# Graph network of two layers: scatters without an order among themselves, list transpositions behind given messages, a small first piece

## The chip, the cores and the metric

The kernel runs on one core of one Trainium2 chip. The metric is the device time of one execution in microseconds (us). PE is the matrix engine, DVE the vector engine, ACT the scalar engine, POOL the general engine that also issues indirect transfers, SP the engine that issues most plain transfers. Each engine works through its own instructions in order and waits on semaphores.

## The reference

There are 6250 nodes with 256 features and 106250 edges, sorted by target; the last edge of each target is its loop. Each edge has one of two kinds. Layer 0 sends a message over each edge, sums the messages at the target, and passes the sum through gates and three small layers; layer 1 is graph attention with four heads. After each, the input is added and the row normalized.

```python
S = feat[src]
def edge_nn(x, W, b):
    h = relu(x @ W.T + b)
    return relu(h @ W.T + b)
msgs = where(rel == r, edge_nn(S, W_rel[r], b_rel[r]), msgs)   # r = 0, 1
agg = segment_sum(msgs, dst)
i, f, g, o = split(agg @ W_ih.T + b_ih + b_hh, 4)
c = sigmoid(i) * tanh(g)
hn = sigmoid(o) * tanh(c)
x0 = layernorm(x + mlp3(hn))
# layer 1: edges and a further loop for each node
h = (x0 @ W).reshape(n, 4, 64)
e = leaky_relu(a_src[src] + a_dst[dst], 0.2)
alpha = exp(e - m[dst]) / (denom[dst] + 1e-16)      # softmax over each target's edges
y = segment_sum(h[src] * alpha, dst) + bias + x0
out = layernorm(x0 + relu(layernorm(y) * gamma + beta))
```

## The kernel before, in words

A message depends only on the source node and the kind of the edge. So the kernel first makes the messages of every node for both kinds, and then gathers them by edge. It has three stages. The line numbers here are those of the kernel before.

**The first stage**, in `gnn_kernel`, does two things at once that do not depend on each other.

*The messages.* The 49 blocks of 128 nodes are taken in chunks of four (line 1132). For a chunk, SP loads the features turned (`fxc`, three buffers), PE does the first stage of the messages (L1143: two kinds, two halves of the features out, two halves in, so eight matmuls over up to 512 columns into `fph`), and ACT writes ReLU of it into `fhT` (L1150). Then for each block PE does four matmuls (L1157) into `fpm`, of which there are two buffers; DVE adds the bias (L1165) into `fms`, of which there are three; ACT takes ReLU (L1168), and SP stores the block in the table `parts` (L1170). The trace records each of these matmuls as two.

*The list.* The gathers need the list of edges without the loops. The edges lie in 7 groups of 126 runs of 128. DVE closes each run up over its loops by shifts of 1, 2, 4 ... 64 places (`frame` and `moved`, lines 878 to 902), and works out where the three blocks of each run go (`place`). POOL scatters them: 7 groups of 3 blocks make 21 indirect transfers into `packed` (L931). SP reads the closed list back from `packed` (`both` and `low_2`, lines 961 to 970, six transfers). DVE takes it apart again (lines 992 to 1048, here called the list operations): source row, target, kind, and the place where a target begins. PE turns five such arrays with 35 transpositions (L1059) and spreads the window's first targets with one matmul (`low_p`, L1085); DVE copies the results into the tables of indices (`idx0`, `idx1`, `mark`, `first`, `slot`).

The order of the instructions on each engine in this stage is set by a scheduler when the program is built: it places the instructions by the dependences that it knows and by costs of its own. Two transfers that write the same array in DRAM are taken to depend on each other, unless the kernel says that they do not.

**The second stage** (`fast`, first half) is layer 0. POOL issues 782 gathers of 128 rows from `parts` (L1265), PE sums them by one-hot matmuls (L1622), and the gates and small layers run beside that, in an order written out by hand. It begins when all messages are stored: on ACT the copy of `mark` (L1643) waits for the stores, and the first gather waits for it.

**The third stage** (`fast`, second half) is the attention: 782 gathers from `rows` in the same way, the weights of the edges, and the sums (L1911). A second path, `general`, for edges that are not sorted, is in the program and is not run with these inputs.

Of the kernel before, what the change touches and what calls it, by code (L numbers as in the profile page):

```python
# [42 lines left out]
P = 128  # L43
# [6 lines left out]
NB = -(-N // P)  # L50
# [6 lines left out]
CHUNK = 4  # L57
# [5 lines left out]
def blocks_of(n, size):  # L63
    return [(i, min(size, n - i)) for i in range(0, n, size)]
BF16 = mybir.dt.bfloat16
WT = 7
TC = -(-(E - N) // P)
NW = -(-TC // WT)
SLOTS = 64
NG = NW // 2  # L70
CT = 18 * WT
# [3 lines left out]
NC = -(-EC // CT)  # L75
# [628 lines left out]
def gnn_kernel(  # L704
# [26 lines left out]
    nc = tc.nc  # L731

    def at(ap, offset, dims):
        return bass.AP(tensor=ap.tensor, offset=ap.offset + offset, ap=dims)

    def rows(ap, n):

        return at(ap, 0, [[0, P], [1, n]])
# [7 lines left out]
    packed = dram.tile([2 * BLOCKS, HB], I32, name="packed")  # L746
# [25 lines left out]
    with (  # L772
# [2 lines left out]
        tc.tile_pool(name="fmsgp", bufs=2, space=PSUM) as mps,  # L775
    ):
        WrT_s = mw.tile([P, 2, 2, D], F32, name="fWrT")
        nc.scalar.dma_start(WrT_s, WrT.rearrange("r (k p) f -> p r k f", p=P))
        brc = mw.tile([P, 2, 2], F32, name="fbrc")
        brr = mw.tile([P, 2 * D], F32, name="fbrr")  # L780
        with nc.allow_non_contiguous_dma(reason="bias vectors, one element a partition"):
            nc.scalar.dma_start(brc, br.rearrange("r (k p) -> p r k", p=P))
        nc.scalar.dma_start(brr, rows(br, 2 * D))
        zrow = mw.tile([1, D], F32, name="fzrow")
        nc.vector.memset(zrow, 0.0)
        nc.sync.dma_start(parts0[ZERO0 : ZERO0 + 1, :], zrow)

        with (
# [19 lines left out]
            rest = EC - (NC - 1) * CT  # L808
            whole = CT * P
# [69 lines left out]
            for b in range(7):  # L879
                s = 1 << b  # L880
# [44 lines left out]
            for b in range(3):  # L925
                nc.vector.tensor_scalar(
                    place[:, b, :], two_t, side, float(b), op0=OP.add, op1=OP.add
                )
            for k in range(NC):
                for b in range(3):  # L930
                    nc.gpsimd.indirect_dma_start(  # L931
                        out=packed,
                        out_offset=bass.IndirectOffsetOnAxis(ap=place[:CT, b, k : k + 1], axis=0),
                        in_=frame[:CT, k, b * HB : (b + 1) * HB],
                        in_offset=None,
                    )


# [15 lines left out]
            both = lp.tile([P, 2, NC, P + 1], I32, name="both")  # L954
            nc.gpsimd.memset(both[:, :, NC - 1, :], 0)
            low_2 = lp.tile([1, 2, NW + 1], I32, name="low_2")
            nc.gpsimd.memset(low_2, 0)
            rest = TC - (NC - 1) * CT
            for s in range(2):
                o = (s * BLOCKS + 1) * HB - 1  # L960
                nc.sync.dma_start(
                    both[:CT, s, : NC - 1, :],
                    at(packed, o, [[P, CT], [whole, NC - 1], [1, P + 1]]),
                )
                nc.sync.dma_start(
                    both[:rest, s, NC - 1, :],
                    at(packed, o + (NC - 1) * whole, [[P, rest], [1, P + 1]]),
                )
                with nc.allow_non_contiguous_dma(reason="the last edge before each window"):
                    nc.sync.dma_start(  # L970
                        low_2[:, s, 1:NW], at(packed, o + WT * P, [[0, 1], [WT * P, NW - 1]])
                    )

            low_r = lp.tile([1, NW + 1], I32, name="low_r")
# [2 lines left out]
            low = lp.tile([1, NW + 1], F32, name="low")  # L977
# [66 lines left out]


            dstE = lp.tile([P, COLS], F32, name="dstE")
            src0 = src1
            nc.vector.tensor_scalar(src0[:CT], src1[:CT], 1.0, None, op0=OP.subtract)
            for to, of in (
                (idx0, row),  # L1050
                (dstE, list_f[:, :, 1:]),
                (mark, rel_f[:, :, :P]),
                (idx1, src0),
                (first, steps),
            ):
                for k0, kn in blocks_of(NC, 4):
                    pt = lps.tile([P, 4 * CT], F32, name="turned")
                    for k in range(kn):
                        nc.tensor.transpose(  # L1059
                            pt[:, k * CT : (k + 1) * CT], of[:CT, k0 + k, :], ident[:CT, :CT]  # L1060
                        )
                    n = min(kn * CT, COLS - k0 * CT)
                    if to is not mark:
                        nc.vector.tensor_copy(to[:, k0 * CT : k0 * CT + n], pt[:, :n])
                        continue

                    to2, of2 = (
                        ap.rearrange("p (g j) -> p g j", j=2 * WT)
                        for ap in (mark[:, k0 * CT : k0 * CT + n], pt[:, :n])
                    )  # L1070
                    for a, b, c in ((0, 1, 0), (1, 2, WT), (2, WT + 1, 1), (WT + 1, 2 * WT, WT + 1)):
                        nc.vector.tensor_copy(to2[:, :, a:b], of2[:, :, c : c + b - a])
            ones = lp.tile([P, P], F32, name="fones")
# [8 lines left out]
            nc.vector.tensor_scalar(odd_i, odd[:, 6:7], 1.0, None, op0=OP.min)  # L1082

            low_p = lps.tile([P, NW + 1], F32, name="low_p", bufs=1)
            nc.tensor.matmul(low_p, ones[0:1, :], low, start=True, stop=True)  # L1085
            low_b = lp.tile([P, NW + 1], F32, name="low_b")
            nc.vector.tensor_copy(low_b, low_p)
            own = dstE[:, : NW * WT].rearrange("p (w j) -> p w j", j=WT)
# [31 lines left out]
            for w0, wn in blocks_of(NW, P // (WT + 1)):  # L1120
                pt = lps.tile([P, 4 * CT], F32, name="turned")
                n = wn * (WT + 1)
# [6 lines left out]
                    slots[w0 : w0 + wn, :].rearrange("w (j e) -> (w j) e", e=P), rel_b[:n, :]  # L1129
                )  # L1130

        for b0, bn in blocks_of(NB, CHUNK):
            cols = bn * P
            xc = mp.tile([P, 2, CHUNK * P], F32, name="fxc", bufs=3)
            nc.sync.dma_start(
                xc[:, :, :cols], xT[:, b0 * P : b0 * P + cols].rearrange("(k p) n -> p k n", p=P)
            )
            hT = mp.tile([P, 2, 2, CHUNK * P], F32, name="fhT")
            for r in range(2):
                for m in range(2):  # L1140
                    ph = mps.tile([P, CHUNK * P], F32, name="fph")
                    for k in range(2):
                        nc.tensor.matmul(  # L1143
                            ph[:, :cols],
                            WrT_s[:, r, k, m * P : (m + 1) * P],
                            xc[:, k, :cols],
                            start=(k == 0),
                            stop=(k == 1),
                        )
                    nc.scalar.activation(  # L1150
                        hT[:, r, m, :cols], ph[:, :cols], AF.Relu, bias=brc[:, r, m : m + 1]
                    )
            for j in range(bn):
                pm = mps.tile([P, 2, D], F32, name="fpm")
                for r in range(2):
                    for k in range(2):
                        nc.tensor.matmul(  # L1157
                            pm[:, r, :],
                            hT[:, r, k, j * P : (j + 1) * P],
                            WrT_s[:, r, k, :],  # L1160
                            start=(k == 0),
                            stop=(k == 1),
                        )
                ms = mp.tile([P, 2, D], F32, name="fms", bufs=3)
                nc.vector.tensor_add(  # L1165
                    ms.rearrange("p r f -> p (r f)"), pm.rearrange("p r f -> p (r f)"), brr
                )
                nc.scalar.activation(ms, ms, AF.Relu)  # L1168
                b = b0 + j
                nc.sync.dma_start(  # L1170
                    parts0[2 * b * P : 2 * (b + 1) * P, :].rearrange("(p r) f -> p (r f)", r=2),
                    ms.rearrange("p r f -> p (r f)"),
                )

    odd_v = nc.values_load_multi_w_load_instructions(
        odd_i,
# [845 lines left out]
```

## Time and profile before

| what | value |
|---|---|
| median of 10 runs | 2275.83 us (2272.63 to 2279.74) |
| the profiled execution | 2274.85 us |
| its span in the trace | 2272.7 us |
| first stage, to the first gather at 204.34 | 204.3 us: PE busy 181.4, DVE 110.8, ACT 68.8, POOL 27.0; granted clock 0.97 |
| second stage, to 1222 | 1017.7 us: PE busy 858.5, DVE 372.6, POOL 751.4; granted clock 0.92 |
| third stage, to the end | 1050.7 us: PE busy 511.7, DVE 752.5, POOL 747.4; granted clock 0.68 |

All times in the text are microseconds from the start of the span. In a line of the trace in order of time, the first number is the start, the second the time to the end of the (merged) instructions, then come engine, line, operation, written and read tile, shapes, and count; in brackets stands how long the engine was idle before, and what ended that. An engine's name with q is its instruction queue, which issues transfers. The time of the profiled execution lies 2.15 above its span: that is outside of what the trace shows. In the slices of the page a digit is the busy share of a fortieth of the span in tenths.

### The profile page before, as it was taken

The numbers are of one execution on the slowest core, as the hardware profiler recorded it, in microseconds if no ns is written. First come the engines' busy times: TensorE is split into PE (matmuls) and PEld (weight loads), VectorE is DVE, ScalarE is ACT, GpSimd is POOL, SyncE is SP. The second block draws the span as 40 slices with busy tenths as digits, with TensorE's granted clock in tenths as the row PEclk, the third lists the DMA queues.
The fourth block names the chain that finished last, engine by engine and source line by source line (L and its number), as shares of the span: only waits on it lengthen the run. The fifth ranks groups of instructions, "written<-read, shape, count | busy, mean of one in ns | idle before, by whom it ended". The sixth has DMA issues, their size and how long they took to land. (4 is left out here: it accounts for less than half of the span.)

```text
span 2272.7 us, 22029 instructions
## 1 busy us (share of the span) xinstructions
PE 1551.6 (68%) x5722; PEld 769.9 (34%) x5722; DVE 1235.9 (54%) x3332; ACT 506.9 (22%) x1525; POOL 1525.8 (67%) x1603
## 2 busy tenths in 40 slices
PE   8987788887888888888992354554545545454563
PEld 5654233333333333333451232222323223232332
DVE  7452134334333343333542577677776877777786
ACT  3322012221222212222342112211111111212111
POOL 1213777777777777777773777777777777777760
PEclk9988799999999899999996676766767677676766
DMA  5335435554455544555553555555555555555550
GB/s 160 123 95 150 134 112 170 167 159 145 143 169 164 158 145 145 168 166 163 172 163 92 144 156 149 154 144 157 152 147 163 145 156 152 149 158 148 151 142 26
DMA packets 163393, 332.53 MB, mean 146 GB/s; under 512 B 42451, under 2 KB 74290, under 8 KB 163257
## 3 DMA queue, kind: packets, MB, share of 16 engines
q0 software_dynamic: 75968, 208.00, 33.6%
q1 hardware_dynamic: 64736, 82.92, 11.3%
q10 hardware_dynamic: 22553, 40.12, 5.7%
q8 instruction: 47, 0.77, 0.1%
q14 instruction: 89, 0.73, 0.1%
HBM read 278.79 MB, written 52.12 MB: 146 GB/s over the span
## 5 line engine op out<-in xcount | busy, mean ns | idle before, releaser
L1265 POOL DMA_INDIRECT G<-parts,fidx x782 | 748.4, 957 | 305.7 <-issue 218.4
L1265 POOL DMA_INDIRECT G<-rows,fidx x782 | 746.5, 955 | 240.6 <-issue 224.2
L1622 PE MATMUL fps<-G,oh 128*64 128x257 f32 (+1 forms) x1674 | 525.6, 428 | 145.9 <-DMA G<-parts,fidx 131.2
L1911 PE MATMUL fps<-gw,oh 128*64 128x264 f32 (+1 forms) x1674 | 437.6, 472 | 232.8 <-DVE gw L1802 232.8
L1911 PEld LDWEIGHTS fps<-gw,oh 128*64 128x64 f32 (+1 forms) x1674 | 230.2, 168 | 409.3 <-DVE gw L1802 250.0
L1622 PEld LDWEIGHTS fps<-G,oh 128*64 128x64 f32 (+1 forms) x1674 | 193.2, 148 | 453.4 <-DMA G<-parts,fidx 232.9
L1802 DVE TENSOR_TENSOR gw<-G,bank 128x1792 f32<-128x1792 f32 (+1 forms) x167 | 249.0, 1491 | 177.9 <-ACT gw L1801 176.9
L1433 DVE TENSOR_SCALAR kind<-fps 128x1 f32<-128x1 f32 x112 | 12.5, 153 | 316.5 <-PE fps L1622 316.5
L1475 PE MATMUL fpg<-faT,fWihT 128*128 128x512 f32 (+2 forms) x432 | 171.5, 521 | 0.0
L1750 PE MATMUL turn<-fident,e 128*120 128x128 f32 (+2 forms) x30 | 13.7, 456 | 224.8 <-ACT e L1944 224.8
L1348 DVE TENSOR_TENSOR oh<-bank,fslot 128x1024 f32<-128x1024 f32 x112 | 135.9, 1214 | 2.2 <-ACT bank L1781 2.2
L1851 ACT ACTIVATE frs<-fmv,eps_c 128x1 f32<-128x1 f32 x112 | 33.0, 295 | 298.8 <-DVE fmv L1850 148.5
L1143 PE MATMUL fph<-fxc,fWrT 128*128 128x512 f32 (+1 forms) x208 | 93.0, 596 | 6.3 <-DMA fWrT<-in_WrT_dram 6.2
L1583 DVE COPY nd<-hr 128x4 f32<-128x4 f32 x56 | 10.7, 191 | 156.8 <-ACT hr L1562 156.8
L1475 PEld LDWEIGHTS fpg<-faT,fWihT 128*128 128x128 f32 x432 | 71.1, 191 | 68.9 <-issue 58.6
L931 POOL DMA_INDIRECT packed<-frame,place x21 | 20.9, 993 | 109.0 <-DVE fms L1165 71.4
L1157 PE MATMUL fpm<-fWrT,fhT 128*128 128x256 f32 x392 | 89.0, 380 | 1.0 <-DVE fms L1165 0.9
L1857 ACT ACTIVATE fy<-fy,frs 128x256 f32<-128x256 f32 x112 | 67.2, 600 | 100.2 <-DVE gw L1796 55.1
L1750 PEld LDWEIGHTS turn<-fident,e 128*120 128x120 f32 (+2 forms) x30 | 5.0, 168 | 239.1 <-ACT e L1944 237.9
L1801 ACT COPY gw<-bank 128x28 f32<-128x28 f32 (+1 forms) x167 | 28.6, 171 | 228.6 <-DMA dB<-slots 103.3
L1157 PEld LDWEIGHTS fpm<-fWrT,fhT 128*128 128x128 f32 x392 | 73.3, 190 | 18.1 <-issue 4.8
L1165 DVE TENSOR_TENSOR fms<-fpm,fbrr 128x512 f32<-128x512 f32 x49 | 33.7, 687 | 76.6 <-PE fpm L1157 75.1
(236 smaller groups left out, 1822.5 us busy)
## 6 DMA issues: line engine op xcount, KB each, us to landing
kept<-keep SPq DMA_DIRECT2D x56, 384.0 KB
k<-kept ACTq DMA_DIRECT2D x56, 384.0 KB
dB<-slots ACTq DMA_DIRECT2D x112, 128.0 KB
loop<-parts SPq DMA_DIRECT2D x110, 128.0 KB
parts<-fms SPq DMA_DIRECT2D x49, 256.0 KB
G<-parts,fidx POOLq DMA_INDIRECT x782
G<-rows,fidx POOLq DMA_INDIRECT x782
rows<-hr SPq DMA_DIRECT2D x110, 65.0 KB
```

The source lines that it names most:

```text
L1143: nc.tensor.matmul(ph[:, :cols], WrT_s[:, r, k, m * P : (m + 1) * P], xc[:, k, :cols], start=(k == 0), stop=(k == 1),)
L1157: nc.tensor.matmul(pm[:, r, :], hT[:, r, k, j * P : (j + 1) * P], WrT_s[:, r, k, :], start=(k == 0), stop=(k == 1),)
L1165: nc.vector.tensor_add(ms.rearrange("p r f -> p (r f)"), pm.rearrange("p r f -> p (r f)"), brr)
L1265: nc.gpsimd.indirect_dma_start(out=to_tile, out_offset=None, in_=table, in_offset=bass.IndirectOffsetOnAxis(ap=idx, axis=0),)
L1348: nc.vector.tensor_tensor(to[:, :nj, :], iota_s[:, None, :].to_broadcast([P, nj, SLOTS]), of[:, :, None].to_broadcast([P, nj, SLOTS]), op= ...
L1475: nc.tensor.matmul(pg[:, :cols], WihT_s[:, k, c * P : (c + 1) * P], aT[:, k, :cols], start=(k == 0), stop=(k == 1),)
L1622: nc.tensor.matmul(sums[g][to, :], ohj, got[t], start=begins, stop=ends)
L1801: nc.scalar.copy(gw[:, :, D:HA], ex[:, o : o + n, :])
L1802: nc.vector.tensor_mul(gw[:, :, :D].rearrange("p j (h f) -> p j h f", h=H), of[:, :n, :D].rearrange("p j (h f) -> p j h f", h=H), ex[:, o ...
L1851: nc.scalar.activation(r, mv[u, k, 1:2], AF.Ln, bias=eps_c[u])
L1857: nc.scalar.activation(y, y, AF.Identity, bias=m, scale=r)
L1911: nc.tensor.matmul(sums[g][to, :], ohj, gw, start=begins, stop=ends)
```

## The change

It has three parts, all in the first stage.

1. The first matrices are loaded in two halves, one for each kind, with the small bias between them; ACT's table of functions is loaded ahead of its first use; and the chunks of messages become one chunk of one block and twelve chunks of four.
2. The 21 scatters are declared independent of each other. Each of the six transfers that read the closed list gets an explicit dependence on all 21 scatters.
3. The transpositions of the five arrays and the matmul of `low_p` are given a dependence, for the order only and without a semaphore, on the last matmul of a message block: `low_p` and the first array behind block 35, the others behind blocks 36 to 39.

In the built program the scatters then wait for DVE's shifts and, from the ninth on, for the scatter eight before. On DVE the list operations stand behind the bias add of block 22 (before: of block 33). SP's transfers that read the list stand behind the store of block 20 (before: of block 31). From the first gather on, the order is the same on all engines.

```diff
-        nc.scalar.dma_start(WrT_s, WrT.rearrange("r (k p) f -> p r k f", p=P))
         brc = mw.tile([P, 2, 2], F32, name="fbrc")
         brr = mw.tile([P, 2 * D], F32, name="fbrr")
-        with nc.allow_non_contiguous_dma(reason="bias vectors, one element a partition"):
-            nc.scalar.dma_start(brc, br.rearrange("r (k p) -> p r k", p=P))
+        for r in range(2):
+            nc.scalar.dma_start(WrT_s[:, r, :, :], WrT[r].rearrange("(k p) f -> p k f", p=P))
+            if r == 0:
+                with nc.allow_non_contiguous_dma(reason="bias vectors, one element a partition"):
+                    nc.scalar.dma_start(brc, br.rearrange("r (k p) -> p r k", p=P))
         nc.scalar.dma_start(brr, rows(br, 2 * D))
+        nc.scalar.preload_act_table_set("exp_and_others")
...
+            moves = []
             for k in range(NC):
                 for b in range(3):
-                    nc.gpsimd.indirect_dma_start(
+                    move = nc.gpsimd.indirect_dma_start(
                         out=packed,
...
                     )
+                    for other in moves:
+                        tc.declare_no_dep(move.ins, other.ins, reason="blocks of their own")
+                    moves.append(move)
+
+            def after_moves(load):
+                for move in moves:
+                    tc.add_manual_dep(
+                        load.ins,
+                        move.ins.name,
+                        mybir.DependencyInfo(
+                            mybir.DependencyClass.Sync, mybir.DependencyReason.DATA
+                        ),
+                        reason="the whole list",
+                    )
...
-                nc.sync.dma_start(
-                    both[:CT, s, : NC - 1, :],
-                    at(packed, o, [[P, CT], [whole, NC - 1], [1, P + 1]]),
+                after_moves(
+                    nc.sync.dma_start(
+                        both[:CT, s, : NC - 1, :],
+                        at(packed, o, [[P, CT], [whole, NC - 1], [1, P + 1]]),
+                    )
                 )
...
+            late, turns = [], 0
...
-                        nc.tensor.transpose(
+                        turn = nc.tensor.transpose(
                             pt[:, k * CT : (k + 1) * CT], of[:CT, k0 + k, :], ident[:CT, :CT]
                         )
+                        late.append((turns // 2, turn))
+                    turns += 1
...
-            nc.tensor.matmul(low_p, ones[0:1, :], low, start=True, stop=True)
+            late.append((0, nc.tensor.matmul(low_p, ones[0:1, :], low, start=True, stop=True)))
...
-        for b0, bn in blocks_of(NB, CHUNK):
+        for b0, bn in [(0, 1)] + [(1 + b, n) for b, n in blocks_of(NB - 1, CHUNK)]:
...
-                        nc.tensor.matmul(
+                        made = nc.tensor.matmul(
                             pm[:, r, :],
...
+                for n, one in late:
+                    if b == NB - 14 + n:
+                        tc.add_manual_dep(
+                            one.ins,
+                            made.ins.name,
+                            mybir.DependencyInfo(
+                                mybir.DependencyClass.NoSync, mybir.DependencyReason.DATA
+                            ),
+                            reason="the list comes late",
+                        )
```

More of the change, by code (lines that the diff above doesn't have):

```diff
@@ L960, in gnn_kernel @@
                 o = (s * BLOCKS + 1) * HB - 1
-                nc.sync.dma_start(
-                    both[:CT, s, : NC - 1, :],
-                    at(packed, o, [[P, CT], [whole, NC - 1], [1, P + 1]]),
-                )
-                nc.sync.dma_start(
-                    both[:rest, s, NC - 1, :],
-                    at(packed, o + (NC - 1) * whole, [[P, rest], [1, P + 1]]),
+                after_moves(
[3 more added lines that the diff above has]
+                    )
+                )
+                after_moves(
+                    nc.sync.dma_start(
+                        both[:rest, s, NC - 1, :],
+                        at(packed, o + (NC - 1) * whole, [[P, rest], [1, P + 1]]),
+                    )
                 )
                 with nc.allow_non_contiguous_dma(reason="the last edge before each window"):
-                    nc.sync.dma_start(
-                        low_2[:, s, 1:NW], at(packed, o + WT * P, [[0, 1], [WT * P, NW - 1]])
+                    after_moves(
+                        nc.sync.dma_start(
+                            low_2[:, s, 1:NW], at(packed, o + WT * P, [[0, 1], [WT * P, NW - 1]])
+                        )
                     )
@@ L1173, in gnn_kernel @@
                 )
+                for n, one in late:
[7 more added lines that the diff above has]
+                            reason="the list comes late",
+                        )
     odd_v = nc.values_load_multi_w_load_instructions(
```

## The prediction

> **What bounds the kernel now.** I read the page first, then the order of time on POOL, PE, DVE and SP in the first 204 us, then the table of busy time by stretches, and beside them the order in which both programs' instructions stand on each engine with the waits that each carries.
>
> The page's slices say where time is made (POOL's busy share, then the granted PE clock):
>
> ```profile
> POOL 1213777777777777777773777777777777777760
> PEclk9988799999999899999996676766767677676766
> ```
>
> From slice 4 on POOL stands at 7 tenths to the end: 782 gathers a layer, 1.25 us apart, with a notch between the layers and a tail. The instruction order of that part is the same in both programs on every engine, so whatever the change does, it does before the first gather, and moves the rest as a block. POOL's scatters, and the first gather:
>
> ```profile
> 78.16 1.16 POOL L931 DMA_INDIRECT packed<-frame,place  x1 [71.37 <-DVE fms L1165]
> 81.15 1.00 POOL L931 DMA_INDIRECT packed<-frame,place  x1 [1.83 <-DMA packed<-frame,place]
> ...
> 135.63 0.98 POOL L931 DMA_INDIRECT packed<-frame,place  x1 [1.51 <-DMA packed<-frame,place]
> 204.34 0.99 POOL L1265 DMA_INDIRECT G<-parts,fidx  x1 [67.73 <-ACT G L1643]
> 205.63 0.96 POOL L1265 DMA_INDIRECT G<-parts,fidx  x1 [0.30 <-DMA packed<-frame,place]
> ```
>
> Each scatter waits for the landing of the one before (57.5 us from first to last, 2.87 apart); a gather follows the last after 0.30. What the first gather waits for is the messages, which are PE's:
>
> ```profile
> 6.19 9.12 PE L1143 MATMUL fph<-fxc,fWrT 128*128 128x512 f32 x16 [6.19 <-DMA fWrT<-in_WrT_dram]
> ...
> 134.06 1.88 PE L1143 MATMUL fph<-fxc,fWrT 128*128 128x512 f32 x4
> 146.90 0.76 PE L1085 MATMUL low_p<-low,fones 1*128 1x113 f32 x2 [10.96 <-DVE low L980]
> 147.59 11.81 PE L1143 MATMUL fph<-fxc,fWrT 128*128 128x512 f32 x20
> ...
> 197.77 1.89 PE L1157 MATMUL fpm<-fWrT,fhT 128*128 128x256 f32 x8
> ```
>
> PE runs without a gap except at the start (6.19), one 0.86, and one 10.96 where a list matmul stands ahead of messages and the list is not there. Its last message ends at 199.66; add, ReLU, store and mark copy take the 4.68 us to the first gather. So: PE's end sets the first gather, and the list sets PE's one stop. The list's own way is on DVE and SP:
>
> ```profile
> 27.19 1.09 DVE L861 SCALAR_TENSOR_TENSOR part_i<-work,fsrc 128x896 int32<-128x896 f32 x1
> ...
> 74.06 1.55 DVE L899 TENSOR_TENSOR frame<-frame,moved 128x1337 int32<-128x1337 int32 x1
> ...
> 143.60 1.10 DVE L992 TENSOR_TENSOR both<-both 126x903 int32<-126x903 int32 x1 [12.04 <-DMA both<-packed]
> ...
> 158.72 0.14 DVE L1043 TENSOR_REDUCE bad<-same 126x1 f32<-126x7 f32 x1
> ```
>
> ```profile
> 137.87 0.35 SPq L961 DMA_DIRECT2D both<-packed  x1
> ```
>
> DVE is full from 27.19 to 77, builds the blocks; SP loads the list 1.26 after the last scatter (135.63 + 0.98); DVE has it 5.73 later and works 15.26 on it without a break.
>
> **The change, part by part.** Times below are of the changed kernel; durations are from the rows above. A chunk of four blocks costs PE 13.77 (chunks start at 92.74, 106.51, 120.29): 8 first-stage matmuls of 0.859 (6.87) and 4 blocks of 1.725. Each matmul is two records.
>
> *Small first piece, split weights, early table.* PE's total stays: the piece of one block, last before (195.30 to 199.66, 4.36), becomes the first. By stretches of half a microsecond, the weights' queue moves its first bytes at 3.0, half of 0.52 MB by 4.7, the last at 5.5, and PE starts 0.7 later. Half the bytes: PE starts at 5.4. Block 0 takes 4.36 and I add 1.3 for the second half of the weights and the slow first matmuls: blocks 1-4 start at 11.1 (9.8 to 12.5). The table load (1.28, before at 7.22 under the first matmuls) was hidden; it stays at nothing, and would cost 1.28 at most.
>
> *Scatters.* In the changed order the first three wait only for the L902 operation (L899 before), the others for the operation behind it (1.1 later, under those three). DVE's list preparation there starts behind the add of block 4. PE gives block 3 at 11.1 + 6.87 + 3 x 1.725 = 23.1; add 0.65, two operations of 1.0, add 0.6: 26.4 where before it was 27.19 (25.0 to 27.8 with the bounds above). From there to the end of L899 before is 75.61 - 27.19 = 48.4, with 12 adds between, and 12 now: 74.8. First scatter 0.95 later as before (77.21 to 78.16): 75.8. A scatter holds POOL 0.98; without the wait the nearest row is the gather's gap, 0.30, so 1.28 apart (the waits left are for the eighth scatter before, 10 us back). Last start 75.8 + 20 x 1.28 = 101.4. The pace is the least known term: no row shows scatters overlapped. Below, 1.25; above, 2.87 if the waits were never the limit. I take 1.28, because the gathers move four times the bytes at 1.25.
>
> [...] In the trace gathers hold 1.25 between 204 and 250 with DVE busy 13.6 of 50. [...]
>
> *The load and what is queued behind it.* SP's list loads now wait for all scatters: 101.4 + 0.98 + 1.26 = 103.6. They stand behind the store of block 20 (about 83), so SP stands still for 20 us with the stores of blocks 21 on behind it. That costs nothing by itself (three message buffers, and DVE is held longer). DVE: in the changed order the 31 list operations stand behind the add of block 22 and ahead of that of block 23. DVE begins at 103.6 + 5.73 = 109.4, is through at 124.6, and has added block 23 at 125.3.
>
> *PE.* Two message banks: block 25 needs the add of block 23. Before it PE can do blocks up to 24 and 13 first-stage matmuls: 11.1 + 5 x 13.77 + 6.87 + 6.9 + 13 x 0.859 = 104.9. So the 10.96 stop ahead of the list matmul goes, and a stop of 20.4 behind DVE comes. The ties do what they say: the transpositions stand behind blocks 35 to 39 and wait for nothing. But the list still holds PE, through DVE's order.
>
> After the stop PE has: 24 blocks x 1.725 = 41.4; 35 first-stage matmuls x 0.859 = 30.1; list matmuls 5 x 0.755 + 0.69 + 0.12 + 0.88 = 5.4; and the slow start after a stop: 10 matmuls from 147.59 to 159.24 took 11.65 where 8.59 is usual, 3.1 (the granted clock is 1.00 from 50 to 100 us and 0.90 from 100 to 150). Sum 80.0. (The same prices give 51.7 for the 52.1 from 147.59 to 199.66 before.) PE ends at 125.3 + 80.0 = 205.3, against 199.66: **+5.6**. The early start is not in this sum except through the 26.4: it only lengthens the stop.
>
> [...]
>
> The tail of 4.68 and the 2068.4 from the first gather to the end stay. The profiled execution took 2274.85, 0.98 under the median of the runs: 2280.5 for its like, and 2275.83 + 5.6 = **2281.4** for the median. From run to run 0.2% (4.6 us) is about what can be told from no change.
>
> **The rivals.**
>
> *The stop is gone, faster.* If the list were through DVE before PE needs block 23's add, PE would run through: 11.1 + 12 x 13.77 + 5.4 = 181.7, that is 18 earlier, 2258. It decides from the point where list operations begin by 88.9 instead of 109.4. At 0.98 of POOL a scatter, 21 of them cannot be over by then; half of it (list 10 us earlier) would be needed for over 0.2%. For it: the ties. Against: DVE's order. 6%.
>
> *About the same.* The chain is 1 to 5 us shorter: pace 1.25 (-0.6), preparation from 25.0 (-1.4), slow start as at the kernel's start, 15.15 - 6.19 - 6.87 = 2.1 (-1.0): +2.6, 2278.4. 24%.
>
> *The scatters go no faster.* If descriptors or landing, and not the order, set 2.87: list 31.8 later, PE ends at 237, 2313. Against: the waits of 1.5 to 3.4 before each scatter are for landing, and go. 6%.
>
> *Forecast:* slower by 3 to 13. 64%.
>
> **How the numbers follow.** Slower by over 0.2% is the forecast and the slow-scatter rival, 0.70; within 0.2% 0.24; faster 0.06. Range: below 2277.5, the short chain with half a microsecond of spread; above 2290, a pace of 1.6 (+6.4) with the late preparation (+1.4). Outside lie the faster case, the slowest scatters and some of the same, about 2 in 10.
>
> **What would show it.** Right: scatters 1.28 apart from 76 to 102; SP's list load near 104; DVE waiting from about 92 to 109, then 15.3 of list work, then block 23's add; PE idle about 20 us to 125, released by that add; no idle before the transpositions; first gather near 210. Wrong: scatters apart by over 1.6; PE released before 115; PE's idle time under 10; a span from first gather to end that differs from 2068 by over 2.

## The result and the profile after

| | before | after |
|---|---|---|
| median | 2276.16 us (28 runs) | 2283.68 us (8 runs, 2282.59 to 2288.41) |
| ratio | | 1.0039, 95% interval 1.0030 to 1.0047 |
| profiled execution | 2274.85 | 2286.18 (span 2284.3) |
| first gather | 204.34 | 214.03 |
| from there to the end of the span | 2068.4 | 2070.3 |

The changed kernel is slower, by 0.39%. Its profiled execution lies 2.5 above its median, the one before 1.3 below, so the two traces stand 11.6 apart and the medians 7.5.

First the slices of the page after, POOL's busy share and the granted PE clock:

```profile
POOL 1301777777777777777773777777777777777760
PEclk9988699999999999989996666767767676676776
```

The shape is that of before: 7 tenths from the fifth slice on. On POOL only the second to the fourth slice differ: the scatters are now packed into a short stretch, and the gathers start a little later. POOL in order of time (start, length, what; idle before and its end in brackets):

```profile
79.00 1.21 POOL L937 DMA_INDIRECT packed<-frame,place  x1 [72.20 <-DVE frame L902]
80.51 0.99 POOL L937 DMA_INDIRECT packed<-frame,place  x1 [0.30 <-issue]
...
105.00 0.98 POOL L937 DMA_INDIRECT packed<-frame,place  x1 [0.30 <-issue]
...
214.03 0.99 POOL L1306 DMA_INDIRECT G<-parts,fidx  x1 [108.05 <-ACT G L1684]
215.32 0.96 POOL L1306 DMA_INDIRECT G<-parts,fidx  x1 [0.31 <-DMA packed<-frame,place]
```

The 21 scatters start 1.30 apart ((105.00 - 79.00) / 20), with 0.30 between them and no wait for a landing: that part of the change does what it says, and ends the scatters at 106 and not at 136.6. Yet the first gather comes 9.69 later than before. It still waits for the messages, PE's, in the same order of time:

```profile
4.70 3.55 PE L1173 MATMUL fph<-fxc,fWrT 128*128 128x128 f32 x16 [4.70 <-DMA fWrT<-in_WrT_dram]
...
24.33 3.23 PE L1187 MATMUL fpm<-fWrT,fhT 128*128 128x256 f32 x8 [2.12 <-DVE fms L1195]
...
97.35 11.32 PE L1173 MATMUL fph<-fxc,fWrT 128*128 128x512 f32 x26
130.07 9.18 PE L1187 MATMUL fpm<-fWrT,fhT 128*128 128x256 f32 x32 [21.39 <-DVE fms L1195]
...
160.61 0.92 PE L1086 MATMUL turned<-fident,frow 126*128 126x126 f32 x7
...
202.32 7.07 PE L1187 MATMUL fpm<-fWrT,fhT 128*128 128x256 f32 x32
```

PE starts 1.5 earlier, has no idle time ahead of the transpositions (160.61), and stands still twice ahead of message matmuls, each time released by DVE's add: for 2.12 at 24.33, and for 21.39, from 108.67 on. The last message ends at 209.39 (before 199.66). Ahead of that add, on DVE:

```profile
28.41 1.08 DVE L864 SCALAR_TENSOR_TENSOR part_i<-work,fsrc 128x896 int32<-128x896 f32 x1
...
76.50 1.55 DVE L902 TENSOR_TENSOR frame<-frame,moved 128x1337 int32<-128x1337 int32 x1
...
94.16 0.69 DVE L1195 TENSOR_TENSOR fms<-fpm,fbrr 128x512 f32<-128x512 f32 x1 [1.09 <-PE fpm L1187]
114.15 1.10 DVE L1018 TENSOR_TENSOR both<-both 126x903 int32<-126x903 int32 x1 [19.30 <-DMA both<-packed]
...
129.28 0.14 DVE L1069 TENSOR_REDUCE bad<-same 126x1 f32<-126x7 f32 x1
129.34 1.27 DVE L1195 TENSOR_TENSOR fms<-fpm,fbrr 128x512 f32<-128x512 f32 x2
```

The add at 94.16 is block 22's; then DVE waits 19.30 for the list, works on it to 129.42, and only then come the adds of blocks 23 and 24 (129.34). SP's queue has the list load in front of the stores in the same way:

```profile
80.47 5.08 SPq L1200 DMA_DIRECT2D parts<-fms  x4
107.92 0.35 SPq L982 DMA_DIRECT2D both<-packed  x1
...
111.94 0.40 SPq L1200 DMA_DIRECT2D parts<-fms  x1
```

The stores of blocks 17 to 20 begin at 80.47; the next store is issued at 111.94, behind the six list loads. This line turned out to matter more than the prediction had it.

### The profile page after: what moved, and what is told of

The parts are those of the page before. It is cut to its first block, busy times and chain, and to the rows that moved or that the text cites. A ratio compares the mean times of both kernels' runs of the same rounds, so it can differ in the third digit from the quotient of the medians.

```text
span 2284.3 us, 22029 instructions
## 1 busy us (share of the span) xinstructions
PE 1550.6 (68%) x5722; PEld 774.4 (34%) x5722; DVE 1237.3 (54%) x3332; ACT 507.0 (22%) x1525; POOL 1525.4 (67%) x1603
## 5 line engine op out<-in xcount | busy, mean ns | idle before, releaser
L1474 DVE TENSOR_SCALAR kind<-fps 128x1 f32<-128x1 f32 x112 | 12.5, 153 | 312.2 <-PE fps L1663 312.2
L1599 PE MATMUL fpg<-Wx,fyT 128*128 128x264 f32 x224 | 72.0, 449 | 0.7 <-ACT fyT L1590 0.7
```

Of the source, the lines that this page charges most:

```text
L1599: nc.tensor.matmul(ph[u, :], hs[i][:, k, u], Wx[:, k, :], start=(k == 0), stop=(k == 1))
```

## The experiments

Each kernel's time is compared with runs of the kernel before that were taken beside it. "First gather" is POOL's first gather in the trace.

| kernel | ratio to before, 95% interval | first gather | PE's stop |
|---|---|---|---|
| small piece only | 1.0002 (0.9992 to 1.0011) | 206.63 | 11.91 |
| scatters only | 1.0026 (1.0017 to 1.0035) | 211.06 | 17.95 |
| no free scatters | 1.0016 (1.0007 to 1.0025) | 208.60 | 16.00 |
| all three parts | 1.0039 (1.0030 to 1.0047) | 214.03 | 21.39 |
| list loads on POOL | 1.0003 (0.9994 to 1.0013) | 214.49 | 21.80 |
| DVE ties only | 1.0021 (1.0011 to 1.0031) | 208.98 | 15.44 |
| both ties, DVE in one piece | 0.9985 (0.9976 to 0.9994) | 200.92 | 5.51 and 2.38 |
| both ties, spread | 0.9980 (0.9971 to 0.9989) | 198.55 | 5.96 |
| list loads on POOL, DVE spread | 0.9946 (0.9932 to 0.9960) | 200.56 | 5.96 |

**Which part costs the time.** Small piece only is the kernel before with part 1; scatters only is the kernel before with part 2; no free scatters is the changed kernel without part 2:

```diff
-                    for other in moves:
-                        tc.declare_no_dep(move.ins, other.ins, reason="blocks of their own")
...
-                after_moves(
-                    nc.sync.dma_start(...)
-                )
+                nc.sync.dma_start(...)
```

Expected of small piece only:

> The kernel before with the first part of the change alone (first piece of one block, split weights, early table). Theory (the list, not PE's start, sets the end): PE starts 1.5 us earlier and reaches its list matmul about 4 us earlier, but the list comes no earlier, and 1 to 2 us later if the relation load lands as late as in the changed kernel; its stop grows by as much as the start gained. After it PE has 22 first-stage matmuls (18.9), 14 blocks (24.2), list matmuls (5.4) and a slow start (3.1): 51.6 from about 149, so messages end near 200.6, +0.9, and the time is 2275 to 2280. Rival (the early start is gained in full): 4 us faster, about 2272.

Measured: no difference (1.0002), PE's stop 11.91, the list 2.76 later than before (146.36 against 143.60), first gather +2.3. PE:

```profile
24.88 2.97 PE L1160 MATMUL fpm<-fWrT,fhT 128*128 128x256 f32 x8 [2.18 <-DVE fms L1168]
...
149.66 0.77 PE L1088 MATMUL low_p<-low,fones 1*128 1x113 f32 x2 [11.91 <-DVE low L983]
```

The time is as expected, the way to it is not. PE did not reach its list matmul 4 earlier but 1.8 later than before (149.66 - 11.91 = 137.75, before 146.90 - 10.96 = 135.94): the early start was lost ahead of it, 2.18 at once in the wait at 24.88. The stop grew by 0.95: the list came 2.76 later, PE 1.8.

Expected of scatters only:

> The kernel before with the second part of the change alone (scatters without an order, list loads behind all of them). In its built order the list matmul stands on PE behind 53 first-stage matmuls and 24 blocks, where PE is at about 97, and the list operations on DVE behind 23 adds. Theory: PE stands still from there until the list is there at about 110 to 113, and again until the row numbers are made near 123; messages end near 209, time 2282 to 2288, as slow as all three parts together, since the loss is this part's. Rival (the ties are what makes it slow): the list is used as soon as it comes and the time is under 2270.

Measured: 1.0026, 2283.5, the stop at the expected place; messages end at 206.38, where 209 was expected. The stop in its trace, PE in order of time:

```profile
92.57 4.46 PE L1164 MATMUL fph<-fxc,fWrT 128*128 128x512 f32 x10
114.97 0.76 PE L1106 MATMUL low_p<-low,fones 1*128 1x113 f32 x2 [17.95 <-DVE low L1001]
...
126.92 0.97 PE L1080 MATMUL turned<-fident,frow 126*128 126x126 f32 x7 [0.35 <-DVE frow L1047]
```

Without the ties the list matmul itself stands in PE's way, released by the list operation that makes `low`; so PE waits for the list though it comes 32 earlier than before, because the scheduler put the list matmul 12 blocks earlier too. The second stop that was expected near 123 is 0.35.

Expected of no free scatters:

> The changed kernel without its second part (scatters ordered as before; small piece and ties stay). The list then begins on DVE near 145, in its built order behind 33 adds, and PE's block 35 waits for the add of block 33 behind it, to about 161.5. After that PE has 12 first-stage matmuls (10.3), 14 blocks (24.2), list matmuls (5.4) and a slow start (3.1): messages end near 204.5, +5 against the kernel before, time 2277 to 2283, between the kernel before and the changed one. Rival (the loss is in the first and third part): as slow as the changed kernel or slower, 2284 and more. Second rival (the ties now cover the list as meant): 2272 or less.

Measured: 2281.57, 1.0016, as expected; first gather 208.60 (+4.3), the stop 16.00 with the list at 144.97, released by the add behind the list:

```profile
160.89 3.78 PE L1163 MATMUL fpm<-fWrT,fhT 128*128 128x256 f32 x8 [16.00 <-DVE fms L1171]
```

Both halves of the change lose alone: with ordered scatters the list stands ahead of the add of block 33, with free ones ahead of block 23's. The sum of 0.16 and 0.26% is about the 0.39% of all three parts; but each stop stands at another place in the order, so no trace shows that they add up.

**Which queue holds PE: DVE's or SP's.** Four kernels with the list loads and the list operations each where the change put them, or out of the way. The ties, added to those that the change has:

```diff
-            nc.vector.tensor_tensor(low_r, ...)         # and the other 30 list operations
+            listed.append(nc.vector.tensor_tensor(low_r, ...))
...
+                ties += [(one, added) for n, one in enumerate(listed) if b == 27 + n // 4]
+                ties += [(one, stored) for one in loads if b == 24]
```

Here `added` is the bias add and `stored` the store of block `b`; the ties are for order only. With both:

> The changed kernel with two more kinds of tie: SP's list loads behind the store of block 24, and DVE's 31 list operations four by four behind the adds of blocks 27 to 34. Theory (the stop is made by where the list stands on DVE): PE runs through. In the changed kernel it had block 24 done at 108.7; the work left took 79.3 there, 77.2 without the slow start after a stop, so its messages end near 186, the first gather comes near 190.5, and the time is about 2261, 0.6% under the kernel before. Rival (the list itself comes too late, wherever it stands): PE stops for over 10 us somewhere between blocks 27 and 36, and the time is within 4 us of the changed kernel's 2284. Second rival (less time before the first gather is given back behind it): first gather near 190, but over 2075 us from there to the end.

Measured: 2272.6, faster than both kernels (0.9980), but by 5.5 and not by 17. The long stop is gone, and another of 5.96 is there:

```profile
111.00 3.60 PE L1177 MATMUL fph<-fxc,fWrT 128*128 128x512 f32 x8
120.55 5.13 PE L1177 MATMUL fph<-fxc,fWrT 128*128 128x512 f32 x8 [5.96 <-ACT fhT L1184]
```

```profile
109.53 0.69 DVE L1199 TENSOR_TENSOR fms<-fpm,fbrr 128x512 f32<-128x512 f32 x1 [1.04 <-PE fpm L1191]
115.52 0.27 DVE L1005 TENSOR_TENSOR low_r<-low 1x113 int32<-1x113 int32 x1 [5.30 <-DMA low<-packed]
...
118.57 0.69 DVE L1199 TENSOR_TENSOR fms<-fpm,fbrr 128x512 f32<-128x512 f32 x1 [2.19 <-DMA parts<-fms]
```

The first add is block 27's, 109.53; the list operations behind it wait to 115.52 for the list, and block 28's add, which could have come at 111.3 (the four adds of a chunk are 1.7 apart), starts at 118.57, last held by a message store that had waited behind the list loads. ACT's ReLU of block 28 stands in order ahead of the ReLU that PE's first-stage matmul needs, so PE stops too. The expectation had misread PE's row: in the changed kernel block 24 was done at 97.4, and what ran to 108.7 were 13 first-stage matmuls ahead of the stop. Here PE has block 28 done at 111.0, and the ties stood a chunk too early.

With the DVE tie alone:

> As the run with both ties, but SP's list loads stay where the changed kernel has them, behind the store of block 20, so that SP stands still from about 83 to 108 with the stores of blocks 21 on behind it. The prediction said that this costs nothing by itself. By that: at most 2 us over the run with both ties (block 24's add waits until about 110.5 for the store of block 21, and PE for it by about 1 us). Rival (a good part of the stop was SP's, through the three message buffers): PE stops by 5 us or more near 110 to 115, and the time is 5 us or more over that run's.

Measured: 2282.12, 9.5 over the run with both ties: the rival holds. The chain, on DVE, ACT and PE:

```profile
96.66 0.69 DVE L1196 TENSOR_TENSOR fms<-fpm,fbrr 128x512 f32<-128x512 f32 x1 [1.03 <-PE fpm L1188]
115.18 0.69 DVE L1196 TENSOR_TENSOR fms<-fpm,fbrr 128x512 f32<-128x512 f32 x1 [17.83 <-DMA parts<-fms]
```

```profile
97.38 0.63 ACT L1199 ACTIVATE fms<-fms 128x512 f32<-128x512 f32 x1 [1.10 <-DVE fms L1196]
115.91 0.63 ACT L1199 ACTIVATE fms<-fms 128x512 f32<-128x512 f32 x1 [17.89 <-DVE fms L1196]
```

```profile
98.13 3.60 PE L1174 MATMUL fph<-fxc,fWrT 128*128 128x512 f32 x8
117.17 5.16 PE L1174 MATMUL fph<-fxc,fWrT 128*128 128x512 f32 x8 [15.44 <-ACT fhT L1181]
```

SP waits for the scatters with its list loads (108.71 to 112.3) and issues the next store at 112.43. The add at 115.18 has waited 17.83 for that store to free one of the three message buffers; ACT's ReLU of the block waits 17.89 for the add, with the ReLUs of the next chunk's first stage queued behind it; PE waits 15.44 for these. So SP's standing still alone makes a stop of 15.44, most of the 21.39.

With the list loads on POOL and DVE's order as the change built it (`nc.sync.dma_start` of the six loads becomes `nc.gpsimd.dma_start`):

> The changed kernel with the six list loads issued by POOL, behind its scatters, and not by SP; DVE's order stays (list operations behind the add of block 22). So SP's stores are never held up, and DVE is. Theory after the runs with ties (either of the two, DVE's order or SP's standing still, stops PE by itself): the list operations begin near 114 to 116 as in the changed kernel, are through near 130, PE stops for about 20 us, first gather near 214, and the time stays within 3 us of the changed kernel's 2284. Rival (the stop was mostly SP's): PE stops for under 12 us and the time is under 2276.

Measured: PE's stop 21.80, first gather 214.49, as expected; DVE's order alone makes the whole stop:

```profile
115.22 1.10 DVE L1018 TENSOR_TENSOR both<-both 126x903 int32<-126x903 int32 x1 [19.71 <-DMA both<-packed]
...
130.41 1.27 DVE L1195 TENSOR_TENSOR fms<-fpm,fbrr 128x512 f32<-128x512 f32 x2
```

The time, though, is 2278.99, 5 under the expected: nothing of that lies before the first gather (see the last section). With the list loads on POOL and the list operations spread:

> The list loads on POOL, and DVE's 31 list operations four by four behind the adds of blocks 27 to 34, so that neither DVE nor SP stands still ahead of message work. Theory: PE has no stop over 1 us after block 4; against the run with both ties, whose messages ended at 193.93, its stop of 5.96 and its slow start of 1.7 go, messages end near 186.3, first gather near 191, time 2259 to 2263, 0.6 to 0.7% under the kernel before. Rival (a third holder behind these two, the feature loads or the message stores themselves): a stop of 4 us or more stays and the time is 2267 or more.

Measured: 2267.04 (5 runs), ratio 0.9946, the fastest of the kernels whose interval is clear of 1; but PE's stop of 5.96 stayed, since the tie is the same: the list came at 118.37, ahead of it block 27's add at 110.23, behind it block 28's at 119.27. First gather 200.56 where 191 was expected: that stop and its slow start, about 9 by the rows (8 records usually take 3.60):

```profile
121.25 6.61 PE L1174 MATMUL fph<-fxc,fWrT 128*128 128x512 f32 x8 [5.96 <-ACT fhT L1181]
```

What is faster here than with both ties is not PE, whose messages end 2.2 later (196.11 against 193.93).

The four rows of this part say: either queue alone stops PE, for 15.4 (SP) or 21.8 (DVE); together they do so once, for 21.4, because they overlap; freeing one gains little or nothing before the first gather (208.98 and 214.49 against 214.03).

**Waiting or working.** Both ties, with all 31 operations behind the add of block 28:

```diff
-                ties += [(one, added) for n, one in enumerate(listed) if b == 27 + n // 4]
+                ties += [(one, added) for one in listed if b == 28]
```

> As the run with both ties, but DVE's 31 list operations stand all behind the add of block 28, in one piece of 15.3 us. If the cost lies in waiting for the list (DVE stood 19.3 us ahead of it in the changed kernel), most of the gain stays: PE has two message banks and up to 12 first-stage matmuls, 13.8 us of work, to do meanwhile, so it stops for 2 to 6 us with its slow start, messages end at 188 to 192 and the time is 2263 to 2267. If the 15.3 us of work in one piece are the cost, PE stops for about 12 and more, and the time is 2273 or more.

Measured: 2274.65, against 2272.6 with the operations spread. The time lies where the second case put it, the stops where neither did. On PE:

```profile
120.79 5.28 PE L1177 MATMUL fph<-fxc,fWrT 128*128 128x512 f32 x8 [5.51 <-ACT fhT L1184]
...
135.33 3.72 PE L1191 MATMUL fpm<-fWrT,fhT 128*128 128x256 f32 x16 [2.38 <-DVE fms L1199]
```

The 15.3 us of list work in one piece cost 2.38 at 135.33, where the two message banks and the first-stage matmuls ran out. The first gather is 2.37 later than with the operations spread (200.92 against 198.55); the time above the first case, as in the run with both ties, comes with the other stop, 5.51, which neither case had. So the greater cost in the changed kernel was waiting: 19.30 ahead of 15.3 of work.

**Later ties, an ordered late list, the relation load.** The last four kernels ran on another chip than the eight above, where the kernel before took 3064.51 (median of 35 runs), 1.35 times the 2278 that it took beside those; the granted clock of the profiled runs was 0.72 and not 0.81, and the gathers waited for other engines (the attention's for DVE by 493 to 516 in all, in the changed kernel's trace by 1.2). Why it is slower there stays open. Their ratios are against that time and none can be told from 1 beyond doubt; what follows rests on their first 210 us.

Later ties (`29 + n // 4`), list loads on POOL:

> The list loads on POOL as before, and DVE's list operations four by four behind the adds of blocks 29 to 36, two blocks later than in the first run with both. There the list had come at 118.4, after the add of block 27 (110.2) and ahead of that of block 28, which so stood 7.3 us late: the tie stood one chunk too early, since PE without a stop has block 28 done at 111 and not block 24. Theory: behind the add of block 29 (about 120) nothing waits; the stop of 5.96 and the slow start of 3.2 go from the messages' end of 196.1 there; they end at 185 to 187, first gather 190 to 191.5. From there to the end the two runs with loads on POOL took 2064 to 2066 (the others 2067 to 2071): time 2256 to 2259, 0.8 to 0.9% under the kernel before. Rival (another holder stays): a stop of 4 us or more, time 2264 or more.

Measured: 0.9993 (0.9965 to 1.0020), first gather 205.99; the expectation failed. The list no longer holds PE for more than 0.89 (ahead of transpositions), but another stop of 7.72 came at 104.2, earlier than the list. DVE ahead of it:

```profile
92.76 0.69 DVE L1196 TENSOR_TENSOR fms<-fpm,fbrr 128x512 f32<-128x512 f32 x1 [7.85 <-PE fpm L1188]
98.03 0.69 DVE L1196 TENSOR_TENSOR fms<-fpm,fbrr 128x512 f32<-128x512 f32 x1 [4.58 <-remote]
109.34 1.29 DVE L1196 TENSOR_TENSOR fms<-fpm,fbrr 128x512 f32<-128x512 f32 x2 [10.62 <-remote]
120.15 0.69 DVE L1196 TENSOR_TENSOR fms<-fpm,fbrr 128x512 f32<-128x512 f32 x1 [9.52 <-PE fpm L1188]
```

Two message adds waited 4.58 and 10.62 for a release that the profile places on no engine ("remote"), while the free scatters were on their way (79.37 to 106.3). On the other chip no such waits stand beside the free scatters: with both ties spread and with the loads on POOL spread, the adds of blocks 21 to 27 waited for PE alone, 1.03 to 1.09 within a chunk. With the old first piece:

> As the run with the later ties, but without the first part of the change (first piece of four blocks, weights in one transfer, the piece of one block last). Theory: now that the list holds nobody, what the first part is worth shows bare. PE starts 1.6 later (6.2 against 4.6), but the start with halved weights has its own wait for the second half (1.1 to 2.3 in the runs) and slow matmuls; counted from the chunk that starts at 92.7 in the kernel before, six chunks of 13.77, 4.36 and 5.4 make 185.1; from the one at 97.2 with the small piece, six chunks and 5.4 make 185.2. So: messages end within 1.5 us of the run with the small piece, the same time within 3 us. Rival (the early start is worth its 1.6 to 4 us once the list is out of the way): 3 us slower or more.

Measured: 0.9981 (0.9950 to 1.0012), first gather 206.97, a like wait of 9.21 and PE's stop of 12.69. With such stops in both, the comparison does not settle what the first part is worth once the list is out of the way; there is no sign that it is worth 3 us. With ordered scatters and a late list (`38 + n // 5`, transpositions at `NB - 5 + n`):

> The scatters in order again (2.9 apart, list on DVE near 148), with the list loads on POOL, DVE's list operations five by five behind the adds of blocks 38 to 44 and the transpositions behind blocks 44 to 48. If the place of the list is all that counts, and not how early it comes, PE runs through here too: its last message near 181, the rest of the list matmuls near 186, the odd flag's chain of small DVE operations behind them, first gather 190 to 196, time 2256 to 2264. Rival (the free scatters are needed for the gain): PE stops ahead of block 38 or the list's end holds the first gather to 204 and more, time 2270 or more.

Measured: 0.9973 (0.9945 to 1.0000), first gather 194.74, within the expected; the expected time, 2256 to 2264, could not be read on this chip. The trace, DVE, PE and POOL:

```profile
148.18 0.69 DVE L1172 TENSOR_TENSOR fms<-fpm,fbrr 128x512 f32<-128x512 f32 x1 [1.09 <-PE fpm L1164]
148.79 0.26 DVE L979 TENSOR_TENSOR low_r<-low 1x113 int32<-1x113 int32 x1
...
163.30 0.68 DVE L1172 TENSOR_TENSOR fms<-fpm,fbrr 128x512 f32<-128x512 f32 x1
```

```profile
164.04 1.99 PE L1164 MATMUL fpm<-fWrT,fhT 128*128 128x256 f32 x8 [0.46 <-DVE fms L1172]
...
182.60 1.89 PE L1164 MATMUL fpm<-fWrT,fhT 128*128 128x256 f32 x8
```

```profile
194.74 1.04 POOL L1284 DMA_INDIRECT G<-parts,fidx  x1 [49.77 <-ACT G L1662]
```

The list comes on DVE at 148.79, 35 later than in the changed kernel, and PE's longest wait from 10 us on to the last message (184.49) is 0.8. No message add waits for "remote" here: from 91 to the end of the scatters DVE is idle for 1.03 to 1.09 between two adds of a chunk, for PE or ACT. So up to the first gather the place of the list in the queues counts for more than how early it comes, and the free scatters were not needed for the gain there; that it shows in the time as well is not shown.

The blanking store behind the relation loads:

> The changed kernel, but the store that blanks the scatters' target is issued by SP behind the relation loads (in the changed kernel ACT issues it 1.9 us earlier than in the kernel before, ahead of them, and the relations come late: list preparation at 28.4 where 26.4 was predicted). Theory: relations land 2 us earlier, and each microsecond goes through the chain list, scatters, list load, DVE, block 23's add, PE: first scatter near 77, first gather near 212, time 1 to 3 us under the changed kernel's 2284. Rival (the relations are late for another reason): list preparation still at 28 or later, no difference.

Measured: 1.0014 (0.9987 to 1.0041); the expected gain on the changed kernel's 2284 could not be read on this chip. The relations land earlier, ACT's copy first:

```profile
20.33 0.94 ACT L850 CAST frel_f<-frel_i 128x903 f32<-128x903 int32 x1 [1.69 <-DMA frel_i<-in_rel_dram]
```

```profile
26.19 1.08 DVE L864 SCALAR_TENSOR_TENSOR part_i<-work,fsrc 128x896 int32<-128x896 f32 x1
```

In the changed kernel these two stand at 22.07 and 28.41: 1.74 and 2.22 later. First scatter 76.07 (79.00), first gather 210.13 (214.03). So the blanking store did stand in the relations' way, by about 1.7 of the 2.0 that the prediction missed. The rest of the 2.22 is the order of this kernel: its list preparation stands ahead of block 4's add (0.60), not behind it. The wait of PE at 24.33 is gone too. The list begins on DVE at 110.85 (114.15) and block 23 is added 3.31 earlier, which is handed on to the first gather; the rest of the 3.9 is a shorter slow start (8.60 against 9.18 for 32 records). PE here stops twice, for 7.34 from 99.5 on, released by ACT's first-stage ReLU, and for 9.07, released by that add.

## Why the prediction was right, and where not

| term | predicted | measured |
|---|---|---|
| PE starts; blocks 1-4 start | 5.4; 11.1 | 4.70; 9.81 |
| list preparation (L864) | 26.4 | 28.41 |
| preparation to the end of L902 | 48.4 | 49.6 |
| pace of the scatters | 1.28 | 1.30 |
| last scatter ends to list load | 1.26 | 1.94 |
| load to list operations; their length | 5.73; 15.2 | 6.23; 15.27 |
| block 23 added | 125.3 | 130.0 |
| PE's stop, from | 104.9 | 108.67 |
| its length | 20.4 | 21.39 |
| PE's work after it | 80.0 | 79.3 |
| PE's last message | 205.3 | 209.39 |
| first gather to the end | 2068.4 | 2070.3 |
| median | 2281.4 | 2283.68 |

**Right: DVE's order alone makes the stop.** The step "the list still holds PE, through DVE's order" is shown by loads on POOL: with SP out of the way the stop is the same (21.80). The ties do what they say, and the stop is there all the same. The rival of a faster kernel needed the list by 88.9 in the built order; no run brought it before 110.

**Near in size, in part by luck.** The sum said +5.6; the first gather moved by 9.69 in the trace and the median by 7.5. The stop's length agrees because both of its ends came 4 to 5 later than predicted. The prediction let the early start go into the stop; it was lost ahead of it. Blocks 1 to 4 began 1.3 sooner than predicted, blocks 5 to 8 began at 27.36 where 24.9 follows from the sum: at 24.33 PE stood 2.12 for an add that on DVE was queued behind an operation waiting for the relations. With the blanking store behind the relation loads that wait is gone, and blocks 5 to 8 begin at 24.66. One sign of being wrong is just touched: from the first gather to the end it is 2070.3, 2.3 over 2068 and 1.9 over the 2068.4 of before.

**Right: the scatters overlap.** 1.30, the row of the gathers (0.30 between two) was the right one. That takes the rival of 2.87 out. Six message adds of 0.68 to 0.69 on DVE lie beside the scatters from 79 to 97, and every scatter behind the first holds POOL for 0.98 to 0.99, with an add beside it or not: these adds cost those scatters nothing that the trace shows.

**Mis-sized: list preparation, by 2.0.** It was taken from PE's block 3 and DVE's adds; the relations were not in that sum at all. ACT issued the blanking store at 13.51 (before 15.41), its first functions having come earlier (the first ReLU at 5.97, before 10.01), and it went out ahead of the relation loads of 14.18 to 15.88. Its 0.88 MB (128 rows of 1728 words) delayed them: ACT stood 4.50 for them, and without the store ahead they were there 1.74 sooner. A part costed at "9.8 to 12.5" for its start had its price on a load that the sum did not name. The rest of the 4.7 at block 23's add is 1.2 on DVE in the preparation, 0.7 ahead of the list load, and half a microsecond each in the pace and in the load's way.

**Wrong: "that costs nothing by itself".** SP's standing still was costed at nothing, with three message buffers and DVE as cover. The cover was DVE's own stop: taken away, SP's stop holds PE for 15.44. The forecast was not hurt, since the two overlap, but a reader who had moved only the list operations on DVE, on the strength of that sentence, would have stayed slower than before (1.0021).

**Too high here: the slow start.** 3.1 was taken from the row of before. After the stop four blocks took 9.01 (130.07 to 139.08) where 6.91 is usual: 2.1; with list loads on POOL 1.7 (8.75 against 7.07), with the DVE tie only 1.6, with both ties 1.5. Two runs stand at the row: 3.0 with loads on POOL spread (6.61 against 3.60) and 2.9 with the later ties (6.47). In the two main traces the granted clock goes with it: in the changed kernel it is 0.50 from 120, still within the stop, to 134, so for PE's first 3.9 us, 0.84 from 134 to 134.5 and 1.00 behind that; before, it is 0.50 for the first 5.1 us (146.9 to 152), 0.60 from 152 to 154 and 1.00 behind that. So 1.5 to 3.1 is what the runs show, and what decides how long the clock stays low is open.

**The threshold held only for the built order.** "It decides from the point where list operations begin by 88.9" is right as long as the adds stand behind the list. With the order changed, a list at 148.8 stopped PE for no more than 0.8.

What stays open: what the message adds' waits for "remote" were. They came on the slower chip and with free scatters only, not with ordered scatters there and not with free ones on the other chip, so the free scatters by themselves do not make them. A run of the later ties where the kernel before takes its usual 2278 was not made.

## What to carry to other kernels

When a result is made to come earlier, look where the scheduler puts its users: here it moved 31 operations and six loads forward with it, ahead of work that was ready, on two in-order queues at once. Before costing one of two waiting queues at nothing, take the other one away in thought and follow the buffers from there; only the kernels that moved both were faster than the one before beyond doubt (0.15 to 0.2%; 0.5% with the loads on POOL, of which 0.3 lie at the very end). A tie that moves the user back, behind work that is ready when the result comes, can be worth more than the earlier result: the first gather came at 194.74 with the list at 148.79, and at 198.55 and 200.56 with the list at 115.52 and 118.37. These are traces from two chips, and the time of the first of them could not be told from the kernel before.

## What the runs showed that was not expected

With the six list loads issued by POOL the span ends sooner after POOL's last scatter of the output. In the kernels with the loads on SP it takes 12.2 to 12.6 us from there to the end of the span (2272.03 to 2284.3 in the changed kernel), in the five with the loads on POOL 4.8 to 5.0 (2273.24 to 2278.2). In both the last bytes move within about 4 us behind that scatter; the rest is a stretch in which the profile shows no work. This is where the kernel with list loads on POOL, its first gather no earlier than the changed kernel's, stands 0.36% better by the ratios (1.0003 against 1.0039). What fills these 7.4 us was not tried.
